# A decoder layer on one core: halves stored by cross attention, a bias as a product, gathers one tile later

## The chip, the cores and the metric

The kernel runs on one core of one Trainium2 chip. Its engines are TensorE (PE, with its weight loads shown apart as PEld), VectorE (DVE), ScalarE (ACT), GpSimd (POOL) and SyncE (SP), which here only issues DMAs. ACT and POOL issue some DMAs too; POOL's are the indirect gathers. Each engine works through its own queue in order, and waits where an instruction's input or buffer is not there yet. The metric is the device time of one execution in microseconds, as a median of several runs.

## The reference

A decoder layer over 16 sequences of 100 tokens (1600 tokens, width 512), in float32: self attention, cross attention to 361 encoder rows per sequence, and a mixture of eight experts of which each token takes two. Each of the three ends in a residual sum and a layer norm.

```python
x = layernorm(x + self_attn(x))                    # 16 heads of 32, causal
q = rmsnorm(x @ Wq + bq)                           # 16 heads of 128
k = rmsnorm(ctx @ Wk + bk); v = ctx @ Wv + bv      # 4 heads of 128, each for 4 of q
p = softmax(q @ k.T * 128**-0.5 + mask)
x = layernorm(x + (p @ v) @ Wo)
logits = x @ router_w + router_b                   # top 2 of 8, softmax of the two
h = silu(x @ expert_w[e] + expert_b[e])            # for the two experts e
y = x + (w1 * h1 + w2 * h2) @ proj_w + proj_b
x = layernorm(x + norm_w * y / rms(y))
```

## The kernel before

Nearly every product is made in three passes: an operand a is split into a high half (a rounded to the fast float32r format) and a low half (a minus the high half), and `mm3` (L145 to L149) adds high x high, high x low and low x high. A `Pair` holds the halves. `split` (L135) makes them: the high half by a cast on ACT (L139) or DVE (L141), the low half by a subtraction on DVE or POOL (L142).

The work goes in stages, in the trace about so: self attention (a, to some 200 us), its output projection, first norm and the queries (b, to some 445), cross attention (c, to some 1077), its output projection with second norm and router (d, first operand loads at 986, last products at 1205), the experts (e), and the combination with projection and last norms (f). Tokens are tiles of 128 (`TT`, thirteen, the last of 64); cross attention goes by sequence b and key head g instead, 64 units of (b, g).

Stage c. Per unit there are four score products (`x_scores`, L788: product, DVE adds the mask and takes the minimum at L798, ACT exponentiates at L809, DVE inverts the sum, POOL scales at L811), three turns of the probabilities (`x_turn`, L814: PE transposes at L819, split by ACT and DVE into pT) and three products with the values (`x_attend`, L823). After the third, ACT evicts the output from PSUM and adds the value bias (L839), and SP stores it into the DRAM tensor `od` (L844), one tile of `od` per token tile, in one or two pieces since 100 does not divide 128. Between these, three of four units project keys and values of the next sequence (`kv_project`, L738, whose squares of K go into a scratch tile sq, L758), and SP fetches queries (qf, L784) and encoder rows (cf, L693). Sixteen times a row of the output weights Wo is fetched (f_wo, L527) and split by ACT and POOL (`load_row`, L518).

Stage d. `parts` (L866) lists 52 parts (t, g): for the first ten tiles t by t, for the last three (TAIL) g by g. `d_load` (L869) loads the part's 128 x 512 operand of from `od` (256 KB, SP) one part ahead, and splits it into ot by ACT and, in turn, POOL or DVE. `d_part` (L878) does its twelve matmuls into acc. After a tile's last part `d_norm` (L898) loads x1, adds, normalises, and stores x2d. One tile later `d_turn` (L980) transposes x2 for the router, and POOL adds the projection's bias pb and SP stores the sum as xbd (L993, L994); `d_logits` makes the router's logits. `load_expert` (L1389) loads the rows of an expert's weights four at a time into slots that have come free (fetch by SP at L1395 through three buffers called stage, split by ACT and POOL). `choose`, `settle` and `slots` (L1110, L1204, L1306) turn logits into a table of 32 slots of 128 tokens of one expert each; they are long chains of small DVE operations.

Stage e. For each slot: POOL gathers its tokens from x2d (`e_gather`, L1348), PE turns them (`e_turn`), a product with weights at a register's address (`e_product`), a bias load by SP (`e_bias`, L1376), DVE's add and ACT's Silu, and a store to ysd (`e_out`, L1378).

Stage f. Per tile: `f_gather` (L1524, two gathers from ysd on POOL), `f_load` (L1545: z from xbd and x2 from x2d), `f_sum` (ACT L1567, DVE L1569), `f_turn`, `f_split`, `f_product` (L1588), `f_square` (L1595: DVE adds z at L1598, ACT squares at L1600, DVE multiplies with the norm's weight at L1604) and the norms (`f_norm`). `TURN` (L1516) names the slot at which a tile's gathers come; `due` (L1764) puts fetch, prepare and project at that slot and the next two, and the norms at the third. Tiles from 9 on (LATE) are done after the last slot, with their loads on ACT's queue.

The order on each queue is not the program's: a planner orders the instructions of all engines by priority (the program's order, unless raised) and by when, in its own model of times, they become ready. What it takes for the time of a load can differ from what the chip takes, and then the queue of that engine stands.

## Time and profile before

| | |
|---|---|
| median of 3 runs | 1408.53 us (1407.09 to 1410.74) |
| profiled execution | 1408.13 us |
| its span, first to last instruction | 1406.4 us |
| mean granted clock of PE | 0.976 |
| PE busy | 1331.6 us, 7928 matmuls |
| DVE, ACT, POOL busy | 942.8, 756.4, 710.3 us |
| moved by DMA | 161.74 MB, 199160 packets |

The profile is of one execution. Its views are: the page (busy times, 40 slices of the span with a digit in tenths, where PEclk is the clock that PE was granted), the waits of an engine (who waited for whom: sum, times, longest), windows (busy time of each engine in a stretch, with the number of its instructions in brackets), the groups of a tile's instructions (durations: shortest/median/longest), and the timeline (start, length, engine, line, what; in square brackets the idle time of the engine before it and what ended that). A busy PE is not PE at its peak, since matmuls overlap in its pipeline: a matmul of 512 columns is shown with some 0.39 us, and the next starts some 0.227 us after it. The kernel's tiles in the trace go by their names without numbers.

### The profile page before, as it was taken

The numbers are of one execution on the slowest core, as the hardware profiler recorded it, in microseconds if no ns is written. First come the engines' busy times: TensorE is split into PE (matmuls) and PEld (weight loads), VectorE is DVE, ScalarE is ACT, GpSimd is POOL, SyncE is SP. The second block draws the span as 40 slices with busy tenths as digits, with TensorE's granted clock in tenths as the row PEclk, the third lists the DMA queues.
The fourth block names the chain that finished last, engine by engine and source line by source line (L and its number), as shares of the span: only waits on it lengthen the run. The fifth ranks groups of instructions, "written<-read, shape, count | busy, mean of one in ns | idle before, by whom it ended". The sixth has DMA issues, their size and how long they took to land.

```text
span 1406.4 us, 25135 instructions
## 1 busy us (share of the span) xinstructions
PE 1331.6 (95%) x7928; PEld 1105.0 (79%) x7928; DVE 942.8 (67%) x2933; ACT 756.4 (54%) x1897; POOL 710.3 (51%) x840
## 2 busy tenths in 40 slices
PE   8999989999999999999999999999999898899894
PEld 7888868888778888888888888878887676677773
DVE  5776677776467777777777767767654558754576
ACT  4666643444446666666666666656654233333356
POOL 6878753344245555555555555545455444532530
PEclk9999989999999999999999999999999999899997
DMA  5221363544442122322233312322446545667883
GB/s 170 68 74 58 124 194 96 131 92 114 100 94 72 42 70 71 76 78 70 71 76 78 74 46 67 73 68 51 118 101 182 178 167 164 211 214 240 256 252 118
DMA packets 199160, 161.74 MB, mean 115 GB/s; under 512 B 133581, under 2 KB 153265, under 8 KB 199029
## 3 DMA queue, kind: packets, MB, share of 16 engines
q1 hardware_dynamic: 189191, 139.77, 36.2%
q0 software_dynamic: 4576, 14.95, 3.4%
q10 hardware_dynamic: 5262, 5.41, 1.3%
q8 instruction: 65, 1.06, 0.3%
q14 instruction: 66, 0.54, 0.1%
HBM read 107.25 MB, written 50.99 MB: 113 GB/s over the span
## 4 chain that ended last, share of the span: by engine, by line
PE 68%; DVE 14%; DMA 7%; ACT 4%; issue 3%; POOL 1%; SPq 1%; ACTq 1%; DVEq 0%; POOLq 0%
PE pq L147 4%; PE pq L148 4%; PE pq L149 4%; PE pv L147 4%; PE pv L148 4%; PE pv L149 4%; PE ptp L819 3%; PE pk L147 3%; PE pk L149 3%; PE pk L148 3%; PE s L147 3%; PE s L148 3%; PE s L149 3%; PE av L148 2%; PE av L147 2%
## 5 line engine op out<-in xcount | busy, mean ns | idle before, releaser
L811 POOL TENSOR_SCALAR p<-p,sums 100x361 f32<-100x361 f32 x256 | 146.4, 577 | 99.4 <-DVE sums L810 88.2
L798 DVE CUSTOM_DVE_ANT_0 p<-s,nmask 100x361 f32<-100x361 f32 x256 | 133.0, 527 | 63.4 <-PE s L149 54.7
L809 ACT ACTIVATE p<-p,nm 100x361 f32<-100x361 f32 x256 | 153.2, 601 | 39.6 <-DVE nm L798 36.3
L142 DVE TENSOR_TENSOR pT_l<-ptp,pT_h 128x400 fp32r<-128x400 f32 (+1 forms) x192 | 107.5, 568 | 57.2 <-ACT pT_h L139 56.8
L147 PE MATMUL pq<-WH 128*128 128x512 f32 (+2 forms) x272 | 107.2, 394 | 5.3 <-DVE WH L141 5.3
L819 PE MATMUL ptp<-ident,p 100*128 100x100 f32 (+1 forms) x768 | 107.4, 252 | 0.0
L139 ACT CAST pT_h<-ptp 128x400 fp32r<-128x400 f32 (+1 forms) x192 | 91.2, 487 | 30.1 <-PE ptp L819 29.7
L142 POOL TENSOR_TENSOR cT_l<-cf,cT_h 128x512 fp32r<-128x512 f32 (+1 forms) x48 | 54.4, 1133 | 103.4 <-ACT cT_h L139 101.5
L819 PEld LDWEIGHTS ptp<-ident,p 100*128 100x128 f32 (+1 forms) x768 | 95.4, 151 | 13.3 <-POOL p L811 2.3
L148 PE MATMUL pq<-WL,WH 128*128 128x512 f32 (+2 forms) x272 | 104.9, 385 | 0.0
L149 PE MATMUL pq<-WH,WL 128*128 128x512 f32 (+2 forms) x272 | 104.6, 385 | 0.0
L149 PE MATMUL acc<-WH,ot_l 128*128 128x512 f32 (+1 forms) x208 | 85.7, 413 | 7.3 <-DVE ot_l L142 5.8
L147 PE MATMUL acc<-WH,ot_h 128*128 128x512 f32 (+1 forms) x208 | 85.1, 409 | 5.0 <-ACT ot_h L139 5.0
L147 PE MATMUL s<-kT_h,WH 128*100 128x362 f32 x256 | 88.1, 355 | 0.7 <-ACT kT_h L139 0.7
L147 PE MATMUL av<-pT_h,WH 128*128 128x400 f32 (+1 forms) x192 | 76.8, 400 | 9.0 <-ACT pT_h L139 8.6
L666 POOL TENSOR_TENSOR qs<-qs,r_q 128x512 f32<-128x512 f32 (+1 forms) x52 | 54.0, 1068 | 60.9 <-DVE r_q L171 49.4
L149 PE MATMUL s<-kT_h,WL 128*100 128x362 f32 x256 | 84.3, 329 | 0.0
L148 PE MATMUL s<-kT_l,WH 128*100 128x362 f32 x256 | 83.7, 327 | 0.0
L148 PE MATMUL acc<-WL,ot_h 128*128 128x512 f32 (+1 forms) x208 | 83.6, 402 | 0.0
L142 POOL TENSOR_TENSOR WL<-qf,WH 128x400 fp32r<-128x400 f32 x64 | 67.3, 1052 | 30.5 <-ACT WH L139 26.9
L147 PE MATMUL pv<-WH,cT_h 128*128 128x512 f32 (+1 forms) x192 | 79.8, 416 | 0.9 <-DVE WL L142 0.9
L148 PE MATMUL pv<-WL,cT_h 128*128 128x512 f32 (+1 forms) x192 | 77.9, 406 | 0.0
(348 smaller groups left out, 3990.6 us busy)
## 6 DMA issues: line engine op xcount, KB each, us to landing
qf<-qd SPq DMA_DIRECT2D x64, 200.0 KB
of<-od SPq DMA_DIRECT2D x48, 256.0 KB
cf<-in_ctxT SPq DMA_DIRECT2D x16, 722.0 KB
eb<-in_expert_b SPq DMA_DIRECT2D x32, 256.0 KB
ysd<-h SPq DMA_DIRECT2D x32, 256.0 KB
f_e<-in_expert_w SPq DMA_DIRECT2D x30, 256.0 KB
f_wq<-in_Wq SPq DMA_DIRECT2D x16, 256.0 KB
f_wo<-in_Wo SPq DMA_DIRECT2D x16, 256.0 KB
```

The source lines that it names most:

```text
L139: ins = nc.scalar.copy(dst.h, src)
L142: low.tensor_tensor(dst.l, src, dst.h.bitcast(FP), ALU.subtract)
L147: nc.tensor.matmul(out, a.h, b.h, start=start, stop=False)
L148: nc.tensor.matmul(out, a.h, b.l, start=False, stop=False)
L149: nc.tensor.matmul(out, a.l, b.h, start=False, stop=stop)
L666: nc.gpsimd.tensor_tensor(qr[:, hs, :], qr[:, hs, :], rs[:n, hs].unsqueeze(2).to_broadcast([n, GR, HD2]), ALU.mult,)
L798: nc.vector.tensor_tensor_reduce(out=p, in0=sc[:, :SE], in1=nmask, scale=1.0, scalar=BIG, op0=ALU.add, op1=ALU.min, accum_out=nm,)
L809: nc.scalar.activation(p, p, AF.Exp, bias=nm, scale=-1.0, accum_out=sh)
L811: nc.gpsimd.tensor_scalar(p, p, sh, 1.0, ALU.mult, ALU.mult)
L819: nc.tensor.transpose(pt[:n, h, :], probs[h][:, c0 : c0 + n], ident[:S, :S])
```

## The change

In cross attention the output leaves PSUM in halves: ACT's eviction writes the high half in float32r, and a new DVE operation reads PSUM again, adds the bias and subtracts the high half. `od` has room for both, and the store moves both. The output projection loads halves straight into its operand (512 KB in place of 256), three parts ahead, with four buffers (every fourth part's from a pool of its own); there is no split. x1 is loaded two parts ahead of the norm. The rows of experts are fetched up to three ahead and split one or two at a part, by a list. To make room, K's squares go to PSUM, the minima of a unit share a tile, the probabilities have eight buffers in place of nine, and some small tiles share tags. The router's weights are loaded at the start of cross attention.

The bias of the projection is no longer added to x2 and kept in DRAM: it is a product of a row of ones with its two halves (33 rows, of which two count), the first matmul of each tile's projection. So xbd goes, with its stores and loads, and x2 is added at L1598's place. In stage f all tiles below LATE fetch, prepare, project and norm one slot later, the older tiles' steps first in each slot.

```diff
-    od = [dram.tile([128, NH, 128], FP, name=f"od_{t}") for t in range(NT)]
+    od = [dram.tile([128, NH, 2, 128], FP, name=f"od_{t}") for t in range(NT)]
...
+    rw = kvk.tile([128, KC, NE], FP, name="rw")
+    nc.scalar.dma_start(rw, router_w.rearrange("(k p) e -> p k e", p=128))
+    rb = kvk.tile([128, NE], FP, name="rb")
+    nc.scalar.dma_start(rb, router_b.partition_broadcast(128))
...
-                out=sq[:n],
+                out=pk[:n, h * HD2 : (h + 1) * HD2],
...
-        p = w1.tile([S, SE], FP, name=f"p2_{n}", tag="p", bufs=9)
-        nm = w3.tile([S, 1], FP, name=f"nm2_{n}", tag="nm", bufs=6)
+        p = w1.tile([S, SE], FP, name=f"p2_{n}", tag="p", bufs=8)
+        nm = nms[:, h : h + 1]
...
-        o = w2.tile([128, GR, S], FP, name=f"o2_{b}_{g}", tag="o")
-        nc.scalar.activation(o, av, AF.Identity, bias=bvT[:, g : g + 1])
+        o = w2.tile([128, GR, 2, S], FR, name=f"o2_{b}_{g}", tag="o")
+        bias = bvT[:, g : g + 1]
+        nc.scalar.activation(o[:, :, 0, :], av, AF.Identity, bias=bias)
+        nc.vector.scalar_tensor_tensor(
+            o[:, :, 1, :],
+            av,
+            bias,
+            o[:, :, 0, :].bitcast(FP),
+            ALU.add,
+            ALU.subtract,
+        )
+        of = o.bitcast(FP)
...
-                od[t][:, g * GR : (g + 1) * GR, r : r + m], o[:, :, a : a + m]
+                od[t][:, g * GR : (g + 1) * GR, :, r : r + m], of[:, :, :, a : a + m]
...
-    def d_load(i):
-        t, g = parts[i]
-        n = TT[t][1]
-        p = inp["d"]
-        of = p.tile([128, GR, 128], FP, name=f"of_{t}_{g}", tag="of")
-        nc.sync.dma_start(of[:, :, :n], od[t][:, g * GR : (g + 1) * GR, :n])
-        OT[t, g] = pair(p, [128, GR, 128], f"ot_{t}_{g}", tag="ot")
-        split(OT[t, g][:, :, :n], of[:, :, :n], low=nc.vector if i % 2 else nc.gpsimd)
+    def d_fetch(upto):
+        for i in range(fetched[0], min(upto, len(parts))):
+            t, g = parts[i]
+            n = TT[t][1]
+            p = inp["d2" if i > HEAD * NKV and i % 4 == 2 else "d"]
+            o = p.tile([128, GR, 2, 128], FR, name=f"ot_{t}_{g}", tag="ot")
+            nc.sync.dma_start(o[:, :, :, :n].bitcast(FP), od[t][:, g * GR : (g + 1) * GR, :, :n])
+            OT[t, g] = Pair(o[:, :, 0, :], o[:, :, 1, :])
+            fetched[0] = i + 1
...
-        nc.gpsimd.tensor_tensor(x2[:n], x2[:n], pb[:n], ALU.add)
-        nc.sync.dma_start(xbd[t][:n], x2[:n])
...
+    BY = (NT - TAIL) * NKV
+    erows = [(e, k) for e in early for k in range(KC)]
+    split_at = [HEAD * NKV + 2 + 2 * r for r in range(len(erows))]
+    assert split_at[-1] < BY + TAIL
+    for g in range(NKV - 1):
+        first = BY + TAIL * (g + 1)
+        erows += [(wo_slot[g], k) for k in range(KC)]
+        split_at += [first + min(k, TAIL - 1) for k in range(KC)]
+    erows += [(wo_slot[-1], k) for k in range(2)]
+    split_at += [len(parts)] * 2
+    rows_in, rows_out = [0], [0]
+    ROWS = 3
+
+    def e_rows(i):
+        while rows_out[0] < len(erows) and split_at[rows_out[0]] <= i:
+            e, k = erows[rows_out[0]]
+            split_row(f"e_{e}", k)
+            rows_out[0] += 1
+            e_fetch()
+
+    def e_fetch():
+        while rows_in[0] < min(rows_out[0] + ROWS, len(erows)):
+            r = rows_in[0]
+            e, k = erows[r]
+            fetch_row(f"e_{e}", e, kp(expert_w[e]), k)
+            rows_in[0] += 1
+
+    e_fetch()
     for i in range(HEAD * NKV, len(parts)):
         t, g = parts[i]
-        if i + 1 < len(parts):
-            d_load(i + 1)
+        d_fetch(i + 4)
+        if g == 2:
+            d_x1(t)
+        e_rows(i)
...
+        f = stage.tile([128, D], FP, name="f_pb", tag="f")
+        b = inp["f1"].tile([33, D], FR, name="pb")
+        nc.gpsimd.memset(f[:33], 0.0)
+        for r in (0, 32):
+            nc.scalar.dma_start(f[r : r + 1], proj_b.rearrange("(o n) -> o n", o=1))
+        nc.scalar.copy(b, f[:33])
+        nc.vector.tensor_tensor(
+            b[32:33], f[32:33], b[32:33].bitcast(FP), ALU.subtract
+        )
+        inp["pb"] = b
+        inp["one"] = inp["f1"].tile([33, 128], FR, name="one_r")
+        nc.gpsimd.memset(inp["one"].bitcast(FP), 1.0)
...
-        for dst, src in ((z, xbd[t]), (x2, x2d[t0 : t0 + n])):
...
+        src = x2d[t0 : t0 + n]
+        if not tail:
+            nc.sync.dma_start(x2[:n], src)
...
-        mmk(pp[:n], lambda f: cp[:, f, :n], lambda f: inp["pw"][:, f, :])
+        nc.tensor.matmul(
+            pp[:n], inp["one"][:, :n], inp["pb"], start=True, stop=False
+        )
+        for f in range(KC):
+            mm3(pp[:n], cp[:, f, :n], inp["pw"][:, f, :], False, f == KC - 1)
...
-        nc.vector.tensor_tensor(y[:n], pp[:n], y[:n], ALU.add)
+        nc.vector.tensor_tensor(y[:n], pp[:n], x2[:n], ALU.add)
...
-                due.setdefault(min(TURN[t] + lag, NSL), []).append((lag, f, t))
+                i = min(TURN[t] + lag + 1, NSL - (lag == 0))
+                due.setdefault(i, []).append((lag, f, t))
     for i in range(FIRST):
-        due.setdefault(TURN[2 * i + 1] + 3, []).append((3, f_norm, i))
+        due.setdefault(TURN[2 * i + 1] + 4, []).append((3, f_norm, i))
...
-        for _, f, t in sorted(due.get(i, []), key=lambda d: d[0]):
+        for _, f, t in sorted(due.get(i, []), key=lambda d: -d[0]):
```

## The prediction

> **What bounds the kernel now.** The page first: who is busy, and when.
>
> ```profile
> PE 1331.6 (95%) x7928; PEld 1105.0 (79%) x7928; DVE 942.8 (67%) x2933; ACT 756.4 (54%) x1897; POOL 710.3 (51%) x840
> ...
> PEclk9999989999999999999999999999999999899997
> DMA  5221363544442122322233312322446545667883
> ```
>
> TensorE (PE) is the bound. Of the span of 1406.4 us it idles 75. So an edit pays only by work taken off PE, by stalls of PE that go, or by lost clock. The waits of PE say which stalls there are; the upper fence is the whole span, in which the av lines belong to cross attention (about 445 to 1077 us), the acc lines to its output projection (993 to 1205).
>
> ```profile
> PE av L147 <- ACT pT_h L139: 8.6, 10, 2.6
> PE acc L149 <- DVE ot_l L142: 5.8, 4, 3.6
> ...
> PE acc L147 <- ACT ot_h L139: 5.0, 2, 3.7
> PE av L148 <- DVE pT_l L142: 3.8, 19, 0.3
> ...
> PE pp L147 <- ACT pp L1600: 2.7, 1, 2.7
> ...
> PE acc L149 <- POOL ot_l L142: 1.4, 2, 1.3
> ```
>
> The acc lines are PE waiting for the split that the change removes: 5.8 + 5.0 + 1.4 = 12.2 us. The table of windows adds what a stall costs beyond itself (columns: stretch, PE, weight load, DVE, ACT, POOL busy, granted clock, DMA share, GB/s):
>
> ```profile
> 1106.00:1110.00 4.00, 1.35 (x4) 0.81 (x5) 1.95 (x5) 1.80 (x4) 3.75 (x3) 0.89 0.46 150
> 1110.00:1114.00 4.00, 4.00 (x18) 3.29 (x16) 3.07 (x6) 1.95 (x5) 4.00 (x4) 0.68 0.36 131
> ...
> 1178.00:1182.00 4.00, 0.85 (x4) 0.37 (x2) 4.00 (x13) 0.62 (x1) 1.15 (x1) 0.85 0.63 223
> 1182.00:1186.00 4.00, 3.55 (x9) 1.96 (x10) 3.79 (x9) 1.50 (x3) 2.24 (x3) 0.50 0.35 98
> 1186.00:1190.00 4.00, 4.00 (x16) 3.06 (x15) 3.83 (x9) 1.00 (x3) 1.71 (x2) 0.80 0.28 77
> ```
>
> After the gaps of 3.65 and 3.60 us the clock falls: 4 x (0.11 + 0.32) = 1.7 us lost, and 4 x (0.15 + 0.50 + 0.20) = 3.4. So the removed wait holds 12.2 + 5.1 = 17.3 us. The Trainium skill, "TensorE: Matmul & The Clock Gate", section "Why this matters for your kernels", wants no idle gaps over some 3 us; by it these two gaps alone would cost clock, yet in this trace one of 2.62 us in cross attention (ended at 931.7) was also followed by 0.50.
>
> In cross attention the tile view of f_wo (the output weights' rows) and two of its lines matter:
>
> ```profile
> L527 SPq DMA_DIRECT2D f_wo<-in_Wo x16: 346/526/1779, 512.4 to 959.3; - x16
> ...
>   DMA f_wo<-in_Wo: 25.3, 16
> ```
>
> ACT waits 16 times, 1.6 us each, for such a row before its cast, and the longest PE stalls there follow these waits (ACT 3.31, PE 2.62; 2.10, 1.43; 2.15, 1.26). In the timeline each row's load is SP's next instruction after an od store. Last, stage e and the tail:
>
> ```profile
> 1299.77 0.94 POOL L1340 DMA_INDIRECT y<-ysd,slot  x1 [11.82 <-DMA ysd<-h]
> ...
> 1305.43 0.72 ACT L1567 ACTIVATE y<-y,g 128x512 f32<-128x512 f32 x1 [4.89 <-DMA y<-ysd,slot]
> ...
> 1367.06 0.69 DVE L1598 TENSOR_TENSOR z<-pp,z 128x512 f32<-128x512 f32 x1 [4.12 <-PE pp L149]
> ```
>
> The first combine gather stands on POOL until a store lands, ACT stands 4.89 us for it, and PE has gaps of 2.96 and 1.06 us up to 1322. At 1367 DVE adds z late; its pp was ready and DMA stood at 0.85 to 0.97, so I read a late load of z.
>
> **The change, part by part.** The sum is made against the profiled execution, 1408.13 us (span 1406.4, 1.7 around it), 0.4 under the median of 1408.53.
>
> *Halves out of PSUM (cross attention).* ACT's 64 evictions stay (594 ns). DVE gains 64 scalar_tensor_tensor of 128x400 from PSUM; the nearest row is pT_l, the same shape and source, 568 ns: 36 us. DVE is busy about 25 of 35 us in these windows, so it goes to about 27. PE's waits for pT_l (3.8 us, 19 times) and pT_h can grow: none if the 10 free us hold it, 29 waits x 0.57 = 16 if each op lands in front of a wait. I take +1.5, near the lower end, because the 19 pT_l waits are 0.16 to 0.25 each.
> The store now waits for DVE too: 0.57 later at best, 1.3 when DVE has a queue (at 923.8 it worked on until 926). Behind it on SP stand f_wo, qf and cf loads. qf and cf are fetched two units ahead (SP itself waits 216 us for their buffers), so they cost nothing; f_wo's wait is ACT's, and then PE's. The store's bytes double: 200 KB filled 2 us at a share of 0.34, 0.7 us of all engines, so another 0.7 ahead of the row. Price: nothing if the order of ACT, which the planner lays out by its own times, moves the cast along; 16 x (0.57 + 0.7) = 20 plus clock at most. I take +4: the later DVE op is in the plan, the transfer hardly, 16 x 0.7 at about a third. The Trainium skill, "DMA: Bandwidth & Descriptors", section "Specifications", speaks against this part: pieces under 512 B are read, modified and written, and these are 400 B, now twice as many. By it the store would move its bytes twice, another 0.7 us at each row, 4 more by my third; no row here shows the reading back.
>
> *Squares of K into PSUM, nm as one tile, p from 9 to 8 buffers.* 152 squares (390 and 365 ns; some are 0.29, some 1.02 us). Without the long ones DVE saves 14 us, with PSUM a tenth of a us dearer it loses 15: 0 on PE, bounds -1 and +2. At most eight p live, since a unit's last transposes come before the next unit's fourth score.
>
> *Loads of halves (output projection).* 52 casts (ACT, 0.62), 26 subtractions on DVE (0.69), 26 on POOL (1.29) go: 32, 18 and 33 us, and with them the 17.3 us. What is late next: DVE's routing chain (it is 3.8 to 4.0 of 4 us busy from 1174 to 1198), which PE needs for the slots at 1198.8; it loses about five ot_l, 4 us, while PE there gains 8.4. So some 4 come back. I take -13; bounds -17.3 and -3.
> New waits: a load of 512 KB waits on SP for part i-1, three parts ahead. Matmuls start 0.227 us apart, so a part is 12 x 0.227 = 2.7 us and the lead 8.2. Behind it on SP stand x1 loads (two parts early), expert rows and x2 stores; DVE's norm and ACT's casts wait for those, PE for neither at once. A 256 KB load took 3.04 us (x1 at worst 5.58); 256 KB more at 320 GB/s add 0.8: 6.4 at worst, under 8.2. Traffic from 1080 to 1200 is 180 GB/s at a share of 0.56; 35 parts add 9.2 MB and ten xbd stores go (2.6), so 235 GB/s and 0.73. +1; bounds 0 and +6.
> The 30 expert rows keep cast (0.62) and subtraction (1.29), now spread and fetched up to three ahead; they no longer stand between a part and its operand, so 0. rw and rb move to the start of cross attention on ACT's queue; the broadcast load of pb (6.23 us) goes: 0, the weight transposes hide it.
>
> *Bias by a product.* 13 adds on POOL (0.9 to 1.3), 13 stores, 13 loads go, 13 matmuls of 128x512 come: 13 x 0.227 = 2.95 on PE. Some lie in the tail where PE idles, so +2.5 (bounds +1 and +3). The eviction still is one add. Its setup (two memsets, two short ACT-queue loads, a cast 0.62, a subtraction 0.69) lies beside stage e: +0.5, bounds 0 and +2.
>
> *Gathers one tile later.* Per tile two gathers (POOL 0.95 each), x2's load on SP, the scale (0.71), sum (0.75), transposes, split and product move behind one more xs gather on POOL and one more eb load and ysd store on SP. The store that the first gather waits for has then landed; with its lost clock (4 x (0.36 + 0.06) = 1.7) the case is worth 2.96 + 1.06 + 1.7 = 5.7. The gather's own 5.6 us stay longer than one slot: -4, bounds -5.7 and +2.
>
> *Tail.* Six z loads on ACT's queue and the last SP ones go, at a DMA share above 0.85. The gap of 2.73 at pp (L147) and 4.12 of DVE's: -3; bounds -5 and +1.
>
> Sum: 1.5 + 4 + 0 - 13 + 1 + 2.5 + 0.5 - 4 - 3 = -10.5. 1408.13 - 10.5 = 1397.6, with 0.4 for the median **1398.0**. Likely between 1390 and 1403.
>
> **Rivals.**
> *The weight rows come late (slower).* Every od store waits on DVE and every row behind it. If ACT's mean wait for f_wo goes from 1.6 to above 2.8 us, PE takes nearly all of it at ten of 16 places (12 us) and half clock at about five (1.7 each, 8.5): +21 in place of +4, so 1415. For it: the pairs of waits above. Against it: the planner moves the cast. It decides from a mean wait of about 2.6.
> *The projection's gain goes elsewhere (no change).* The routing chain on DVE or loads of 512 KB end last: -13 becomes -3, so 1408. For it: DVE at 4.0 of 4 from 1174. Against it: 26 of its operations go.
> *All stalls go.* -17.3, -5.7 and -5, with 0 in cross attention and +2.5 for the product: -25.5, so 1383. Against it: PE must then find everything else early.
> *Halves loaded but hidden anyway*: ot's splits would be off the path; the 12.2 us of PE waits speak against it, so no chance of its own.
>
> **How the numbers follow.** Forecast 0.45, rows late 0.25, gain swallowed 0.15, all stalls go 0.15. 0.3% is 4.2 us, about what a measurement of this kernel can tell from no change: faster (under 1404.3) 0.45 + 0.15 = 0.60, within 0.15, slower 0.25. The range goes from just under the third rival's 1383 to just over the first's 1415: 1381 to 1416.
>
> **What would show it.** Right: no PE wait on ot; granted clock 1.0 from 1090 to 1190; ACT's wait for f_wo under 2.3 us each; DVE about 27 of 35 us in cross attention; 13 bias products 0.23 apart from their neighbours; no POOL wait near 12 us. Wrong: rows of f_wo above 2.6 us with half clock after them, acc matmuls waiting for od's loads, or PE idle before the slots' products as DVE settles.

## The result: slower by 3.5%, and the profile after

The changed kernel takes 1458.66 us in the median of four runs (1457.15 to 1461.93); the kernel before, run beside it, took 1409.63. The ratio is 1.0351, with a 95% interval of 1.0323 to 1.0379: 49 us slower, where 10 us faster was forecast. The profiled execution took 1461.93 us, of which 1460.2 are the span.

The page of the changed kernel first: busy times, and the slices of the span for the granted clock and the DMA share.

```profile
PE 1350.7 (92%) x7941; PEld 1118.4 (77%) x7941; DVE 958.6 (66%) x2972; ACT 729.6 (50%) x1846; POOL 662.6 (45%) x803
...
PEclk9999989999999999999999999999999998998868
DMA  5222363544422333323333333424487773667332
```

Compare the right end with the one before: there the last two slices stood at a clock of 9 and 7, here at 6 and 8, after an 8, and DMA falls to 3 and 2 where it stood at 8 and 3. The tail is longer and emptier. PE idles 109.5 us of the span in place of 75.

To find the place, take the same four moments from both traces: the last store of cross attention's output, the last acc product, the last product of the experts (ph), and the end of the span.

| moment | before, us | after, us |
|---|---|---|
| last od store | 1077.1 | 1076.6 |
| last acc product | 1205.2 | 1215.3 |
| last ph product | 1355.2 | 1366.4 |
| end of span | 1406.4 | 1460.2 |
| from the last ph to the end | 51.2 | 93.8 |

So 43 of the 54 us of span come after the experts, in the combination, and the other 11 before it: the changed kernel is 10 us behind when the output projection ends. The waits of PE over the whole span name what stands there:

```profile
PE av L148 <- DVE pT_l L142: 13.3, 16, 1.1
PE ptc L1630 <- DVE sq L1733: 11.7, 2, 5.9
PE ptp L823 <- DVE kT_l L142: 8.6, 8, 1.2
...
PE acc L147 <- DMA ot<-od: 5.0, 2, 3.1
PE pp L1644 <- ACT pp L1656: 4.6, 3, 1.5
```

The splits of ot are gone from the list, as forecast. New are stalls for pT_l and kT_l, both low halves that DVE makes in cross attention (pT_l had 3.8 us before and kT_l was not there), and longer stalls of the combination's transposes, ptc, behind a norm (3.0 us before). The output projection itself, in four windows of 25 us (columns as in the tables of before: PE, weight load, DVE, ACT, POOL busy, granted clock, DMA share, GB/s), could not be better (before, PE was busy 19.47, 24.78, 23.90 and 20.03 us of these 25, at a clock of 0.93, 1.00, 1.00 and 0.86):

```profile
1090.00:1115.00 25.00, 25.00 (x124) 20.42 (x124) 10.62 (x39) 4.74 (x12) 3.88 (x3) 1.00 0.73 250
1115.00:1140.00 25.00, 25.00 (x126) 20.84 (x125) 7.83 (x31) 4.48 (x10) 5.06 (x4) 1.00 0.78 252
1140.00:1165.00 25.00, 25.00 (x118) 20.16 (x119) 10.69 (x47) 3.09 (x8) 2.54 (x2) 1.00 0.74 249
1165.00:1190.00 25.00, 25.00 (x124) 19.74 (x123) 11.11 (x54) 4.04 (x9) 3.84 (x3) 1.00 0.66 202
```

The tail is the opposite. The timeline of ACT in the changed kernel, cut to the rows that matter (start, duration, then in brackets what the engine waited for before it): L1656 squares one tile's result, L1619 scales the next tile's gathered rows, the first step of its sum.

```profile
1373.59 0.60 ACT L1656 ACTIVATE pp<-z 128x512 f32<-128x512 f32 x1 [4.10 <-DVE z L1654]
...
1374.22 0.71 ACT L1619 ACTIVATE y<-y,g 128x512 f32<-128x512 f32 x1
1377.04 0.59 ACT L139 CAST cp_h<-ptc 128x512 fp32r<-128x512 f32 x1 [2.11 <-PE ptc L1630]
1383.47 0.60 ACT L1656 ACTIVATE pp<-z 128x512 f32<-128x512 f32 x1 [5.84 <-DVE z L1654]
...
1387.53 1.52 ACT L1749 ACTIVATE z<-z,m,r_f 128x512 f32<-128x512 f32 x2 [3.34 <-DVE m L1748]
1388.95 0.70 ACT L1619 ACTIVATE y<-y,g 128x512 f32<-128x512 f32 x1
```

Read it as one queue. ACT stands 4.10 us for DVE to add tile t's product (z), squares it, and only then scales tile t+1. That scale sets off the sum, the transposes, the cast at 1377.04, the product, the add, and ACT stands again, 5.84 us, for its result. In these rows one tile is in work at a time. At every second tile a norm stands in front as well (L1749, 3.34 us). In the kernel before, ACT scaled two tiles ahead of a square (L1567 is the scale there, L1600 the square):

```profile
1354.39 0.71 ACT L1567 ACTIVATE y<-y,g 128x512 f32<-128x512 f32 x1
...
1357.12 0.71 ACT L1567 ACTIVATE y<-y,g 128x512 f32<-128x512 f32 x1
...
1359.73 0.61 ACT L1600 ACTIVATE pp<-z 128x512 f32<-128x512 f32 x1
```

DVE's adds of the tiles follow at 1372.9, 1382.7, 1397.0, 1406.8 and 1420.9, so 10 and 14 us apart; in the tail of the kernel before, they came 3 to 8 us apart. When the experts ended, five tiles had been added before and two in the changed kernel. The clock is lower too. First the changed kernel, then two stretches of the tail before:

```profile
1376.00:1386.00 10.00, 6.48 (x17) 4.33 (x17) 3.01 (x11) 1.31 (x3) 1.90 (x2) 0.67 0.18 52
1386.00:1396.00 10.00, 4.68 (x13) 3.55 (x14) 4.49 (x18) 4.86 (x9) 1.90 (x2) 0.52 0.45 157
1396.00:1406.00 10.00, 6.68 (x20) 4.58 (x19) 3.58 (x8) 1.92 (x4) 5.58 (x6) 0.66 0.41 112
```

```profile
1366.00:1376.00 10.00, 6.03 (x22) 4.54 (x22) 7.79 (x29) 6.41 (x15) 0.00 (x0) 0.83 0.83 270
1376.00:1386.00 10.00, 6.69 (x33) 4.83 (x31) 9.11 (x37) 7.61 (x18) 0.00 (x0) 0.98 0.36 115
```

PE's busy share does not tell the two apart: 6.48 and 6.68 us of 10 came with a clock of 0.67 and 0.66, and 6.69 us with 0.98.

By 2 us windows, each with its idle time and what its clock lost, PE's losses by stage are as follows (us; before, then after): cross attention, 420 to 1078: 15.6 + 5.1 and 31.6 + 10.2. Output projection, from 1078: 12.9 + 5.1 and 4.2 + 3.4. Experts: 11.7 + 10.2 and 18.1 + 15.3. After them: 20.6 + 8.5 and 40.7 + 23.6. The loss in cross attention shows in the first acc product, at 1011.2 in place of 993.2, and not in the last od store, beside which the projection already runs.

### The profile page after: what moved, and what is told of

Its sections match the earlier page's. It is cut to its first block, busy times and chain, and to the rows that moved or that the text cites. A ratio compares the mean times of both kernels' runs of the same rounds, so it can differ in the third digit from the quotient of the medians.

```text
span 1460.2 us, 25118 instructions
## 1 busy us (share of the span) xinstructions
PE 1350.7 (92%) x7941; PEld 1118.4 (77%) x7941; DVE 958.6 (66%) x2972; ACT 729.6 (50%) x1846; POOL 662.6 (45%) x803
## 4 chain that ended last, share of the span: by engine, by line
PE 76%; DVE 12%; DMA 4%; issue 3%; ACT 3%; SPq 1%; POOL 0%; DVEq 0%; ACTq 0%; POOLq 0%
PE pq L147 4%; PE pq L149 4%; PE pq L148 4%; PE pk L147 4%; PE pk L149 4%; PE pk L148 4%; PE pv L147 4%; PE pv L149 4%; PE pv L148 4%; PE ptp L823 3%; PE acc L147 3%; PE acc L148 3%; PE acc L149 3%; PE s L148 2%; PE av L148 2%
## 5 line engine op out<-in xcount | busy, mean ns | idle before, releaser
L142 DVE TENSOR_TENSOR pT_l<-ptp,pT_h 128x400 fp32r<-128x400 f32 (+1 forms) x192 | 107.3, 568 | 18.8 <-ACT pT_h L139 18.3
L823 PE MATMUL ptp<-ident,p 100*128 100x100 f32 (+1 forms) x768 | 103.6, 253 | 9.2 <-DVE kT_l L142 8.6
L823 PEld LDWEIGHTS ptp<-ident,p 100*128 100x128 f32 (+1 forms) x768 | 93.2, 153 | 18.1 <-issue 5.4
L147 PE MATMUL acc<-WH,ot 128*128 128x512 f32 (+1 forms) x208 | 84.7, 407 | 5.1 <-DMA ot<-od 5.0
L142 POOL TENSOR_TENSOR WL<-f_e,WH 128x512 fp32r<-128x512 f32 x29 | 38.4, 1339 | 106.3 <-ACT WH L139 81.0
L148 PE MATMUL av<-pT_l,WH 128*128 128x400 f32 (+1 forms) x192 | 71.5, 372 | 14.4 <-DVE pT_l L142 13.3
L148 PE MATMUL acc<-WL,ot 128*128 128x512 f32 (+1 forms) x208 | 83.9, 403 | 0.0
L149 PE MATMUL acc<-WH,ot 128*128 128x512 f32 (+1 forms) x208 | 83.7, 403 | 0.0
L147 PE MATMUL pk<-WH,cT_h 128*128 128x512 f32 (+1 forms) x192 | 79.9, 416 | 0.0
L149 PE MATMUL pk<-WH,cT_l 128*128 128x512 f32 (+1 forms) x192 | 78.2, 407 | 0.0
```

The source lines that it names most:

```text
L142: low.tensor_tensor(dst.l, src, dst.h.bitcast(FP), ALU.subtract)
L147: nc.tensor.matmul(out, a.h, b.h, start=start, stop=False)
L148: nc.tensor.matmul(out, a.h, b.l, start=False, stop=False)
L149: nc.tensor.matmul(out, a.l, b.h, start=False, stop=stop)
L823: nc.tensor.transpose(pt[:n, h, :], probs[h][:, c0 : c0 + n], ident[:S, :S])
```

## The experiments

Chips differ: the kernel before took 1408 to 1416 us on those used here. So the ratios to the kernel before on the same chip are compared; 1% is 14 us.

**The order of the combination.** The changed kernel shifts each tile's steps by one slot, and within a slot takes the larger lag first: norm, project, prepare, fetch. These were undone one at a time and together.

```diff
-        for _, f, t in sorted(due.get(i, []), key=lambda d: -d[0]):
+        for _, f, t in sorted(due.get(i, []), key=lambda d: d[0]):
```

> Kernel: the changed kernel, in which the steps due at one slot are again taken with the smaller lag first (fetch, prepare, project, norm); the shift by one slot stays. Theory A (the reversed order makes the tail serial: the sum of tile t+1 stands on ACT behind the square of tile t, so sum, transposes, split, product, add and square of one tile follow one another): the span from the last product of stage e to the end goes from 93.8 us to 50 to 62, by the end of stage e five tiles instead of two are squared, and the kernel takes 1415 to 1430 us. Theory B (the shift by one slot alone leaves too much work for the tail): 1450 to 1460, two or three tiles squared by the end of stage e. Theory C (x2 wanted at the square, with three stage buffers, or the bias products hold PE): 1445 to 1460, with DVE's add waiting for DMA or PE's product for its bank.

Measured 1.0106 (1.0081 to 1.0131): 2.45% back, 35 us. From the last ph to the end it takes 57 us, within theory A's 50 to 62; four tiles were added by then, not five.

```diff
-                i = min(TURN[t] + lag + 1, NSL - (lag == 0))
+                i = min(TURN[t] + lag, NSL)
...
-        due.setdefault(TURN[2 * i + 1] + 4, []).append((3, f_norm, i))
+        due.setdefault(TURN[2 * i + 1] + 3, []).append((3, f_norm, i))
```

> Kernel: the changed kernel, in which each tile's fetch, prepare, project and norm are due at the slots of the kernel before (no shift by one); the reversed order within a slot stays. Theory A (the reversed order): a serial tail stays, though each step begins a slot earlier; 1435 to 1455 us. Theory B (the shift alone): 1415 to 1430 us, and the tail 50 to 62 us. Theory C (x2 at the square or the bias products): 1445 to 1460.

Measured 1.0276 (1.0215 to 1.0337), 0.75% better than the changed kernel, with the serial tail still there: adds at 1376.0, 1390.1, 1403.1, 1417.8. That rules out theory B. At 1455.6 us it lies just above A's range and inside C's, which the next run decides.

> Kernel: the changed kernel with both the slots and the order of the kernel before; bias product, x2 at the square, squares of K, halves and spread rows stay. Theories A and B: 1412 to 1425 us, of which the 19 to 22 us lost in cross attention are the larger part and the 10 to 12 gained in the output projection are kept. Theory C: above 1440, the tail above 75 us.

Measured 1.0072 (1.0048 to 1.0096), and 53 us from the last ph to the end, about as before; at 1427.8 us it is 3 us above the range of A and B, and far from C's. So order and slots together cost 2.8%, 39 us, and theory C falls: x2 at the square and the bias products have no part in the long tail.

Does it need anything else of the change? The same slots and order were put into the kernel before, alone:

> Kernel: the kernel before, in which only the combine's steps are moved: due one slot later, and within a slot the larger lag first, as in the changed kernel. Theory A (the order alone makes the tail serial): 1.020 to 1.032 of before, the span after the last product of stage e from 51 us to 80 or more. Rival C (it takes x2 at the square or the bias products as well): 0.998 to 1.010.

Measured 1.0252 (1.0214 to 1.0290), 35 us, and 96 us from the last ph to the end. PE's waits in that run show the same lines at the top as the changed kernel's tail (L1578 is ptc there):

```profile
PE ptc L1578 <- DVE sq L1677: 15.9, 2, 8.0
...
PE ptc L1578 <- DVE nm L1667: 7.7, 2, 4.7
```

Next, the narrow form of the theory. The scale of the sum is pinned to its place in the program's order, so a reversed program puts it behind the square. Only the pin was taken away; slots and reversed order stayed.

```diff
-        tc.keep_in_program_order(in_turn(ins, acted[0]))
+        in_turn(ins, acted[0])
```

> Kernel: the changed kernel, slots and reversed order as they are, with one thing taken away: the scale of a gathered row on ACT (the first step of f_sum) is no longer held to its place in program order, so that the planner may set it ahead of the square of the tile before. Theory A in its narrow form (f_sum of tile t+1 stands in ACT's queue behind the square of tile t, which waits for that tile's product): most of the order's price comes back, 1.010 to 1.020 of before (the changed kernel is 1.035), five tiles or more squared by the end of stage e. Rival (it is the norms set ahead of everything else, or the slots): 1.028 to 1.036.

Measured 1.0148 (1.0119 to 1.0177): 2.0 of the 2.45 points come back through one pin, and four tiles were added by the end of the experts. In its timeline ACT now scales well ahead of the squares, and hardly stands for DVE's add:

```profile
1342.69 0.60 ACT L1656 ACTIVATE pp<-z 128x512 f32<-128x512 f32 x1 [0.31 <-DVE z L1654]
...
1344.81 0.71 ACT L1619 ACTIVATE y<-y,g 128x512 f32<-128x512 f32 x1
1350.27 0.60 ACT L1656 ACTIVATE pp<-z 128x512 f32<-128x512 f32 x1 [0.31 <-DVE z L1654]
```

The last of this group keeps norm first and sets the other three right:

```diff
-        for _, f, t in sorted(due.get(i, []), key=lambda d: -d[0]):
+        for _, f, t in sorted(due.get(i, []), key=lambda d: (d[0] < 3, d[0])):
```

> Kernel: the changed kernel with its slots, in which only the norm of earlier tiles is taken ahead of the others at a slot, and then fetch, prepare, project by the smaller lag. If the price of the order is project ahead of prepare: 1.010 to 1.016 of before. If it is the norm ahead of prepare: 1.028 to 1.036.

Measured 1.0221 (1.0172 to 1.0270), between the two expectations. The norm ahead of the others costs 1.15% by itself, the reversed order of those three another 1.3%. Both put work in front of the same pinned scale.

**DVE's low half in cross attention.** First the operation was taken away, with the rest of the changed kernel as it is:

```diff
-        nc.vector.scalar_tensor_tensor(
-            o[:, :, 1, :], av, bias, o[:, :, 0, :].bitcast(FP), ALU.add, ALU.subtract,
-        )
+        nc.gpsimd.memset(o[:, :, 1, :].bitcast(FP), 0.0)
```

> Kernel: the changed kernel, in which the low half of cross attention's output is not computed but set to zero on POOL, ahead of time; it leaves out the 64 operations of DVE that read PSUM, and its output lacks the low halves. Same stores, same bytes. Theory D (those 64 operations make DVE late for the low halves of the probabilities and of K's transposes, on which PE waits about 1 us at a time and then loses clock): cross attention shortens by 14 to 22 us, the waits of PE for pT_l and kT_l go from 13.3 and 8.6 us to under 6 and 3; 1438 to 1448 us. Rival E (the doubled stores and the rows behind them): PE's idle time in cross attention stays within 3 us, 1455 to 1462.

Measured 1.0191 (1.0132 to 1.0250), against 1.0351. By the traces cross attention ends 14 us sooner (last od store 1062.7) and the span is 16 us shorter; the same edit on the kernel with order and slots of before (below) shortens the span by 16 us too. But PE's waits only fell part of the way, not to under 6 and 3:

```profile
PE av L148 <- DVE pT_l L142: 8.1, 14, 1.0
...
PE ptp L823 <- DVE kT_l L142: 7.0, 13, 1.2
```

Then the operation alone, added to the kernel before, into a tile that nobody reads:

```diff
+        ol = w1.tile([128, GR, S], FR, name=f"ol2_{b}_{g}", tag="ol2")
+        nc.vector.scalar_tensor_tensor(
+            ol, av, bvT[:, g : g + 1], o, ALU.add, ALU.subtract
+        )
...
-        p = w1.tile([S, SE], FP, name=f"p2_{n}", tag="p", bufs=9)
+        p = w1.tile([S, SE], FP, name=f"p2_{n}", tag="p", bufs=8)
```

> Kernel: the kernel before with one thing added: 64 operations of DVE in cross attention that compute the low half of each output from PSUM into a tile that nobody reads (p has eight buffers instead of nine, to make room). Nothing is left out. Theory D (that operation alone, in DVE's order, costs cross attention its time): 1.008 to 1.016 of before, PE's waits for pT_l up from 3.8 us to 8 or more. Rival E (the doubled stores, or squares of K in PSUM, cost it): 0.999 to 1.004.

Measured 1.0086 (1.0056 to 1.0117), 12 us. PE's waits within cross attention:

```profile
PE av L147 <- ACT pT_h L139: 14.3, 10, 2.4
PE av L148 <- DVE pT_l L142: 8.6, 14, 1.1
```

In the kernel before these were 8.6 and 3.8. The run has eight buffers for the probabilities in place of nine; the runs that take the operation away keep eight, so the price is the operation's. PE's losses in cross attention go from 15.6 + 5.1 us to 25.7 + 18.8, and more of that is clock than idle time. The 64 operations take 628 ns each, 40 us of a DVE that was free for 28% of the time; they still reach PE, which waits for one result of DVE's queue after another. What such a stall does in the changed kernel is seen at 534 us. The two rows of PE, then the windows:

```profile
533.96 0.54 PE L823 MATMUL ptp<-ident,p 100*128 100x100 f32 x4 [1.18 <-DVE kT_l L142]
535.71 0.70 PE L148 MATMUL av<-pT_l,WH 128*128 128x400 f32 x1 [1.01 <-DVE pT_l L142]
```

```profile
532.00:534.00 2.00, 0.82 (x8) 0.62 (x7) 2.00 (x9) 2.00 (x7) 2.00 (x5) 1.00 0.66 267
534.00:536.00 2.00, 0.99 (x6) 0.73 (x7) 2.00 (x11) 1.08 (x4) 0.95 (x3) 0.88 0.38 89
536.00:538.00 2.00, 2.00 (x8) 1.91 (x8) 0.81 (x5) 0.90 (x3) 0.39 (x1) 0.50 0.99 209
538.00:540.00 2.00, 2.00 (x8) 1.58 (x7) 0.81 (x3) 0.00 (x0) 1.04 (x1) 0.77 0.08 17
```

DVE is at 2.00 of 2. Two gaps of 1.18 and 1.01 us, 1.7 us apart, are followed by half clock: 2 x (0.12 + 0.50 + 0.23) = 1.7 us more.

**Can the low half be made elsewhere?** In the next kernel (order and slots as before) ACT evicts the output as float32, casts it to the high half, and POOL subtracts.

```diff
-        nc.scalar.activation(o[:, :, 0, :], av, AF.Identity, bias=bias)
-        nc.vector.scalar_tensor_tensor(
...
+        of = w1.tile([128, GR, S], FP, name=f"of2_{b}_{g}", tag="of2")
+        nc.scalar.activation(of, av, AF.Identity, bias=bvT[:, g : g + 1])
+        o = w2.tile([128, GR, 2, S], FR, name=f"o2_{b}_{g}", tag="o", bufs=1)
+        split(Pair(o[:, :, 0, :], o[:, :, 1, :]), of, low=nc.gpsimd)
```

> Kernel: the changed kernel with the slots and the order of the kernel before (1.0072 of before, by the third run), in which DVE no longer reads cross attention's output from PSUM: ACT evicts it once as float32, then casts it to the high half, and POOL subtracts it to give the low half, both from SBUF; o has one buffer instead of two. Theory D (DVE's 64 operations cost cross attention 14 to 22 us): 0.988 to 0.998 of before, PE's waits for pT_l and kT_l together under 15 us instead of 21.9. Rival F (ACT's 64 more passes of about 0.6 us take the place of DVE's): PE waits for pT_h above 8 us, 1.003 or more. Rival G (the stores, later by POOL's 1.05 us each, are what counts): 1.005 or more with ACT's or PE's waits on DMA longer.

Measured 1.0159 (1.0117 to 1.0201): worse than with DVE's operation (1.0072), and not for either rival's reason, since PE's wait for pT_h is 0.7 us and for ot's loads 0.4. DVE lost its 35 us of low halves and was as busy as with them: 448 us from 420 to 1010, as in the changed kernel. Its operations on K had grown. The next run shows how.

```diff
-                out=pk[:n, h * HD2 : (h + 1) * HD2],
+                out=sq[:n],
```

> Kernel: the one above (low halves on POOL, slots and order of before) with the squares of K written to SBUF as in the kernel before. Theory H (writing them to PSUM costs DVE 0.06 us more per accumulator read and holds the bank of pk until the squares are done): 3 to 6 us faster than the one above, 0.984 to 0.995 of before. Rival (the squares are beside other work): within 2 us of it.

Measured 1.0116 (1.0076 to 1.0157), overlapping the run above, so theory H is not decided by it. But here the squares have both their operands and their result in SBUF. Three of DVE's squares, and then POOL's operations at the same times, from the two timelines:

```profile
566.21 0.29 DVE L762 CUSTOM_DVE_ANT_0 ksq<-ks 105x128 f32<-105x128 f32 x1
...
566.91 1.24 DVE L762 CUSTOM_DVE_ANT_0 ksq<-ks 105x128 f32<-105x128 f32 x1
...
576.36 1.18 DVE L762 CUSTOM_DVE_ANT_0 ksq<-ks 128x128 f32<-128x128 f32 x1
```

```profile
566.96 1.05 POOL L142 TENSOR_TENSOR o<-of,o 128x400 fp32r<-128x400 f32 x1
...
576.35 1.04 POOL L142 TENSOR_TENSOR o<-of,o 128x400 fp32r<-128x400 f32 x1
```

A square of 0.29 us takes 1.2 when it falls on a subtraction of POOL. By the overlaps in the two timelines from 500 to 700 us, 17 squares that met a two-operand operation of POOL took 0.87 us in the mean, 43 others 0.33; the small operations on K's scales 0.96 (18) and 0.16 (42). The Trainium skill says as much: in "GPSIMD Engine Reference", section "1. Specifications", POOL's access to SBUF is shared with VectorE and contends with DVE instructions that have two SBUF inputs. The kernel before has it too, at fewer places: there 7 squares met such an operation and took 0.84 us, 56 others 0.33. So the half of the time in which POOL is idle is not free for DVE's work.

**What is left of cross attention's loss.** The kernel with order and slots of before, without the operation:

> Kernel: the changed kernel with the slots and the order of before, and with the low half of cross attention's output set to zero on POOL ahead of time instead of computed on DVE; it leaves out the 64 operations, and its output lacks the low halves. If the terms add up (order and slots -2.8%, the operation -1.6%): 0.988 to 0.995 of before, which is what the rest of the change is worth: halves loaded, bias product, spread rows. If the gain of the loads is given back at the routing chain whatever comes earlier: 0.997 to 1.003.

Measured 0.9985 (0.9968 to 1.0003). It is in the second expectation's range: the rest of the change is worth next to nothing. Cross attention still lost 24.3 + 10.3 us to its end at 1066, against 15.6 + 5.1 to 1078 before. One suspect was the zeroing on POOL, which the next run does without:

```diff
+    o_two = [w1.tile([128, GR, 2, S], FR, name=f"o2_{k}") for k in range(2)]
+    for o in o_two:
+        nc.gpsimd.memset(o[:, :, 1, :].bitcast(FP), 0.0)
...
-        nc.gpsimd.memset(o[:, :, 1, :].bitcast(FP), 0.0)
+        o = o_two[g % 2]
```

> Kernel: the changed kernel with the slots and the order of before, without DVE's 64 low halves, and with no work in their place: the output goes into two standing buffers, whose low halves were zeroed once at the start (it leaves the low halves out). Theory J (in the run before of this kind the 64 zeroings on POOL, 0.43 us each, took part of the gain, since DVE's small operations on K's scales grew from 0.20 to 0.60 us beside POOL's work): PE idle and lost clock in cross attention fall by 4 to 8 us from 34.6 us, 0.990 to 0.995 of before. Rival K (what is left is the doubled stores, the squares of K in PSUM or the shorter lead of the output projection): within 0.2% of the 0.9985 of that run.

Measured 1.0005 (0.9980 to 1.0030), cross attention at 21.8 + 9.1 to 1066: theory J falls. Two parts of the change were then put into the kernel before alone, the squares of K in PSUM

```diff
-                out=sq[:n],
+                out=pk[:n, h * HD2 : (h + 1) * HD2],
```

> Kernel: the kernel before, with one part of the change: the squares of K go to PSUM, in place of SBUF. Nothing is left out. Theory H (each accumulator read is 0.06 us dearer, and the bank of the product of K is held until the squares are done): 1.002 to 1.005 of before, PE's waits on kss 1 to 3 us. Rival (beside other work, or gained back since PSUM does not meet POOL's traffic): 0.998 to 1.001.

which gave 1.0053 (1.0028 to 1.0078), 7.5 us, with 27.8 + 5.1 us lost in cross attention, which ends at 1092 here. PE's wait for pT_l went from 3.8 to 7.3 us and 14.5 us of waits for kT_l came up; kss is not among them, so the reason in theory H is not shown, only its price. And the doubled stores, on top of it and then alone (a standing buffer whose second half is zeros):

```diff
+    o_two = [w1.tile([128, GR, 2, S], FR, name=f"o2_{k}") for k in range(1)]
...
-                od[t][:, g * GR : (g + 1) * GR, r : r + m], o[:, :, a : a + m]
+                od[t][:, g * GR : (g + 1) * GR, :, r : r + m], of[:, :, :, a : a + m]
```

> Kernel: the one above, in which cross attention's output is also stored with as many zeros again beside it (a standing buffer; od twice as large, the loads read only the first half): the doubled stores alone. Nothing is left out. If the doubled bytes in front of the weight rows cost: 0.3 to 0.6% over the one above, ACT's wait for the rows up from 25 us. If not: within 0.15% of it.

> Kernel: the kernel before with the doubled stores alone (as many zeros stored beside each output, from one standing buffer; the loads read only the first half); the squares of K stay in SBUF; nothing is left out. If the squares in PSUM cost 0.5% and the stores nothing or less (the planner then sets the rows' casts later on ACT): 0.988 to 0.996 of before, ACT's wait for the rows under 15 us. Rival (my term of the forecast: the stores put the rows off): 1.002 to 1.006, ACT's wait for the rows above 25 us.

Measured 0.9961 (0.9938 to 0.9984) and 0.9955 (0.9930 to 0.9980). Both are faster than the kernel before, so the doubled stores cost nothing; the first, 0.9% under the run with the squares alone, meets neither of its expectations. The second, which stores 64 blocks of zeros to no purpose, is 6 us faster than the kernel before. The pair also says something on the squares of K: with doubled stores, as the changed kernel has them, squares in PSUM or in SBUF make no difference (0.9961 and 0.9955). And the run with the squares alone and the one with both have about the same waits for pT_l and kT_l in cross attention, 21.8 and 20.2 us, though they are 13 us apart, so these waits are not the price; ACT's wait for the weight rows, 36.7 and 11.9 us, does differ. In the page's count of HBM traffic the doubled stores add 13.1 MB written (64.09 for 50.99) and nothing read (107.25 in both), so no reading back shows there. PE's waits within the second run's cross attention:

```profile
PE av L148 <- DVE pT_l L142: 4.4, 23, 0.3
PE av L147 <- ACT pT_h L139: 1.4, 6, 0.3
```

The 8.6 us of PE's wait for pT_h are nearly gone, and so is ACT's for the weight rows: 5.4 us in place of 25.3. Its losses to 1078 are 13.5 + 2.8 in place of 15.6 + 5.1; to its last od store, at 1065, they are 8.0 us and no clock. Most of that gain goes in the output projection, which lost 19.1 + 10.2 in place of 12.9 + 5.1. The rows' casts start 3.5 to 5.2 us after their loads' issue, as before (3.7 to 5.8), so ACT has other work in front of them now. I take it that the planner allows more time for a store of twice the size; the run shows the waits, not the planner's reason. An attempt to get this on purpose fetched each row a unit ahead of its cast:

```diff
-            load_row(f"wo_{w}", wo_slot[w], Wo4[w], k)
+            fetch_row(f"wo_{w}", wo_slot[w], Wo4[w], k)
+        if i % 3 == 0 and 9 <= i < 9 + 3 * NKV * KC:
+            w, k = divmod((i - 9) // 3, KC)
+            split_row(f"wo_{w}", k)
```

> Kernel: the kernel before, in which each row of the output weights is fetched one unit of cross attention (about 10 us) ahead of its cast, in place of just ahead of it; nothing is left out. Theory L (ACT's waits for these rows, 25.3 us in 16, lead to PE's longest stalls and lost clock in cross attention): ACT's wait for the rows goes under 5 us, PE's idle time and lost clock in cross attention from 20.7 us to 10 to 15, 0.993 to 0.997 of before, and so faster than both kernels. Rival (those waits are hidden, or other stalls take their place): 0.999 to 1.003.

Measured 1.0010 (0.9985 to 1.0034), with ACT's wait for the rows at 30.4 us. It tells nothing on theory L: the planner still set each cast 4 to 6 us after its load's issue, so the wait it was meant to remove stayed.

**Output projection and bias.** The kernel before, with loads and splits two parts ahead:

```diff
-        if i + 1 < len(parts):
-            d_load(i + 1)
+        d_ahead(i + 3)
...
+        p = inp["d2" if i > HEAD * NKV and i % 3 == 2 else "d"]
         OT[t, g] = pair(p, [128, GR, 128], f"ot_{t}_{g}", tag="ot")
```

> Kernel: the kernel before, in which the output projection's loads and splits are issued two parts ahead instead of one, with a third buffer for the halves; nothing else is changed, nothing is left out. Theory I (PE's waits on ot are a matter of lead, not of the splits' work): the waits of 12.2 us go to under 5, and 0.991 to 0.997 of before, some of it given back at the routing chain. Rival (the splits' engine time is what is short, DVE being busy 3.8 to 4.0 of 4 us there): waits within 3 us of 12.2, 0.998 to 1.002.

Measured 1.0011 (0.9993 to 1.0029). The waits on ot went from 12.2 to 9.4 us, and the first ph came at 1222.7, 14 us later than in the kernel before and 14 after the last acc product, with new waits for the gathered rows xs (8.6 us). Both numbers of the rival are met, the waits within 3 us and the time; its reason, the splits' engine time, is not shown by that.

And the bias left out, on the changed kernel with order and slots of before:

```diff
-        nc.tensor.matmul(
-            pp[:n], inp["one"][:, :n], inp["pb"], start=True, stop=False
-        )
```

> Kernel: the changed kernel with the slots and the order of before (1.0072), without the 13 products that add the projection's bias; it leaves the bias out. If each product costs its 0.227 us and no more: 2 to 4 us less, 1.004 to 1.006. If the bias products also hold a bank of PSUM and PE's place (PE waits 1.5 to 4 us at a time for ACT's square to free the bank): 6 to 10 us less, 1.000 to 1.003.

Measured 1.0032 (1.0017 to 1.0047) against 1.0072 with the products. That is 5.6 us, by the two intervals 2 to 10, so it does not tell 13 x 0.227 us from a held bank.

## Why the prediction was wrong

*The step that failed is "Gathers one tile later", -4 with bounds of -5.7 and +2.* Slots and order cost +39 us in the changed kernel, +35 alone. The working followed the gather past other work on POOL and SP, and did ask what moves with it, but it read the change as a delay of one slot. It did not ask what the reversed order within a slot puts in front of what on ACT. The runs showed, in place of a wait of 5.7 us that goes, a tail that grows from 51 to 94 us. The pinned scale behind a square that waits for PE is one line of `due` and one of `f_sum`, and the forecast named neither. No rival covered it: with this one term at its measured 35 to 39, the sum goes to +29 to +33, on the slower side.

*DVE's low half: +1.5, bounds 0 and 16.* Measured +12 alone. The upper bound's mechanism was right (an operation ahead of each wait). The choice near the lower end, "because the 19 pT_l waits are 0.16 to 0.25 each", was not: with the operation added, 14 waits were up to 1.1 us. It also took 568 ns for what took 628, and left out the clock, of which that run lost 13.7 us more in cross attention.

*Squares of K: 0, bounds -1 and +2.* Alone in the kernel before +7.5 (4 to 11), outside the bounds; beside doubled stores, as in the changed kernel, +1 (-4 to +6), which agrees with them. The busy time of DVE from 420 to 1078 indeed did not change (459 and 461 us). So the price goes with what else stands in the queues; what it consists of stays open. (There are 192 squares; the forecast's 152 are those from 460 to 960.)

*The weight rows: +4, rival +21 and 0.25 of the chance.* Wrong in sign. The doubled stores alone gave -6 us. In the changed kernel ACT waited 6.4 us for the rows, seven times 0.9, far from the mean of 2.6 at which the rival decides. The argument against it, that the planner moves the cast, fits this; no run tests it. Nor does a run show the reading back of short pieces that the forecast weighed.

*Loads of halves: -13.* Right in mechanism and place: PE busy 25.00 of 25 us at clock 1.00 from 1090 to 1190, and PE's losses in the stage fall from 18.0 to 7.6 us, so -10.4, though two loads at its start came late (5.0 us of waits, a sign that was named as wrong). But the gain did not stay. In the kernel before, PE went from its last acc product to the first ph in 3.7 us, and in 3 to 4 us in every run that had its projection unchanged. In the changed kernel and every run with the loaded halves it took 11 to 14 us. The rows of the changed kernel, whose first ph comes at 1226.2, show it waiting on the routing chain:

```profile
1218.58 0.63 PE L1371 MATMUL pte<-ident,xs 128*128 128x128 f32 x4 [1.17 <-ACT x2f L1009]
1221.46 0.97 PE L1002 MATMUL ptx<-ident,x 128*128 128x128 f32 x4 [2.25 <-DVE one L1140]
```

That is the rival "the projection's gain goes elsewhere", which was priced at the right size, -13 to -3, and given 0.15. The run at 0.9985 and the one with more lead at 1.0011 agree with it; no run isolates the chain.

*Bias product +2.5 and setup +0.5.* Measured 5.6, between 2 and 10: not contradicted. Not forecast was that the planner sets the product early, where it waits 1.54 us at a time for its bank in the tail.

*Tail -3.* The z loads are gone and the tail is no shorter for it: 53 us with the order mended, 51.2 before.

Parts added or undone alone sum to 35 (order and slots) + 12 (operation) + 7.5 (squares) - 6 (stores) + 5.6 (bias), and by the traces - 10 + 8 (projection and what follows it), about 52; with squares and stores measured together (-5.5) it is 45. The whole is 49. The agreement is better than the terms deserve, since each has some 3 us of interval or more and, as the squares show, one edit changes what another costs.

Of the signs to look for, these came as said: no wait on ot's splits, full clock from 1090 to 1190, f_wo under 2.3 us, DVE at 26.6 of 35 us in cross attention. Against it stood the loads of od, PE's idle time before the slots' products, the bias products' places, and POOL, which waited 9.8 us for the first gather as before (11.82) and then up to 17.4 us more for buffers that the late sums held.

## What to carry to other kernels

When a change reorders steps, write down for each in-order queue what now stands in front of what, and what the one in front waits for; here one pinned instruction behind a waiting one made the tail serial, on an engine that was busy a third of the time. Price an operation on an engine with slack by who waits for that engine's next result, not by the slack. A stage that gets faster only pays as far as what stands behind it is ready: here most of the projection's 10 us were given back before the first product of the experts. And a part's price, measured alone, need not hold beside another part: the squares of K cost 7.5 us alone and about 1 beside the doubled stores.

## What the runs showed of the hardware

- DVE operations with SBUF operands took about as long as the two-operand POOL operation that they met: 0.33 us became 0.87, 0.16 became 0.96. Taking 35 us of operations from DVE and giving POOL 59 us (56 subtractions of 1.05 us) left DVE as busy as it was.
- Gaps of 1.18 and 1.01 us close together were followed by a granted clock of 0.50. The Trainium skill, "TensorE: Matmul & The Clock Gate", section "Why this matters for your kernels", wants no idle gaps over some 3 us. In this trace much shorter ones in a pair cost clock, and the measurement decides.
- Twice the bytes in cross attention's stores, still in pieces of at most 400 B, cost no time that a run showed (0.9955 of the kernel before).
